# Half blocks for the experts' last tokens, a table laid over partitions, and new tile pools in a two-layer attention and mixture-of-experts kernel

## The chip, the cores and the metric

The kernel runs on one core of one Trainium2 chip. The metric is the device time in microseconds. Before the change three runs took 1161.4, 1163.57 and 1163.4 us, a median of 1163.4.

## What is computed

Two layers over `x` of 4 x 1024 tokens with 256 features, all in float32. The first adds causal attention and a dense feed-forward part. The second adds a grouped attention (with `qk`, `v`, a gate and rotated heads) and a mixture of 8 experts, of which each token takes 2. The part that the change is about, cut from the reference:

```python
scores = jax.nn.softmax(xf @ Wg.T, axis=-1)
expert_weights, expert_indices = jax.lax.top_k(scores, K)          # K = 2 of E = 8
expert_weights = expert_weights / expert_weights.sum(-1, keepdims=True)
gates = (jax.nn.one_hot(expert_indices, E) * expert_weights[..., None]).sum(axis=1)
h1 = _lora_in(xf, W1, b1, A1, B1)       # 256 -> 512
h3 = _lora_in(xf, W3, b3, A3, B3)       # 256 -> 512
g = jax.nn.silu(h1) * h3
y_e = _lora_out(g, W2, b2, A2, B2)      # 512 -> 256
y = jnp.einsum('te,ted->td', gates, y_e)
...
x = x + _L0_attn_ref(xn, ...) + _L0_ffn_ref(xn, ...)
xn = _layernorm(x, axis=-1)
x = x + _L1_attn_ref(xn, ...) + _L1_ffn_ref(xn, ...)
```

The kernel computes an expert only for the tokens routed to it: 8192 pairs of token and expert.

## The kernel before

The program has three stages in time. Names and lines are those of the profile.

**First layer** (0 to about 528 us): 16 units `u` of 256 tokens go through norms, `scores`, `hidden`, `weighted` and `finish`. Beside them `merge` folds each expert's low-rank parts into its weights, in DRAM (`wm13`, `wm2`). `norms` writes each unit's rows for the experts into a tile `xr` (five buffers of the pool `l0a`), `route` and `send` choose the two experts and each row's place, and `rows_out` (L641) has GpSimd scatter the rows from `xr` into `xg` in DRAM by indirect DMA, 64 of them; the last four are those of the last unit. Expert `e` owns rows `e * RS` and up of `xg`.

**Experts** (588 to 961 us): `table` (L736) counts each expert's tokens on all partitions at once, zeroes the 256 rows behind each expert's last one, and works out in a row of 39 numbers which expert (`etab`) and which rows (`rtab`) each block of `TB` = 256 tokens takes; it also turns each token's two ranks into its rows of the result (`slot1`, `slot2`). With 8192 pairs and 8 experts at most 39 blocks can be needed. `blocks` (L846) runs the first `NSURE` = 36 always and the last 3 under a branch on `live`. Per block, `rows` (L792) reads the row number into a register of ScalarE and fetches the tokens by four DMAs on ScalarE's queue, `weights` (L802) does so for the 1.7 MB of weights on SyncE's, `turn` (L810) transposes on VectorE, `up` (L815) and `down` (L836) multiply, and the result goes to `yg` in DRAM. The matmuls of block `i + 1`'s `up` stand ahead of those of block `i`'s `down`. In `up` the weights are stationary and the tokens stream, 256 columns a matmul; in `down` 128 tokens are stationary and the 256 columns of `w2` stream. A float32 matmul gives two records in the trace.

**Second layer's attention**, one batch of 1024 tokens after the other: `tokens` (L908) loads the normalised input, `heads` (L918) makes and rotates the four heads on VectorE, `values` (L950) and `gates` (L1012) multiply, `groups` (L967) transposes the heads and makes the attention matrices `attnT` and the linear part `linkv`, `gated` (L1034) combines them and `project` (L1061) ends it. Batch 0 runs ahead of the experts, between the first layer's last unit and the first block, with the tiles of pools named `tmp0`, `mid0`, `big0` and `late0`; batches 1 to 3 run behind the experts. `gather` has GpSimd fetch the expert results by `slot1` and `slot2`, `combine` adds them.

The order of the instructions is that of a scheduler that keeps the order of the program within what data, `issue_after` and buffers demand, engine by engine. A pool's tiles take the SBUF addresses of pools that were closed before; with `reuse_waits="tile"` a tile's first write then waits for whatever still uses the old tiles at its addresses, tile by tile. In `values` the matmuls of batch 0 go through two PSUM banks (`p_a`), and VectorE adds the bias and frees the bank.

Of the kernel before, what the change touches and what calls it, by code (L numbers as in the profile page):

```python
# [17 lines left out]
P = 128  # L18
# [33 lines left out]

TB = 256
RS = B * N + TB
NPAIR = 2 * B * N
NBLK = NPAIR // TB + E - 1

NSURE = NPAIR // TB + E // 2
# [4 lines left out]
def block_kernel(ctx: ExitStack, tc: tile.TileContext, x, wq, wk, wv, wfc, w1, w2, wqk, wvl, wg,  # L63
# [52 lines left out]
    for e in range(E):  # L116
# [9 lines left out]

    blkn = pers.tile([P, NBLK], F32, name="blkn")
    nc.gpsimd.iota(blkn, pattern=[[1, NBLK]], base=0, channel_multiplier=0,
                   allow_small_or_imprecise_dtypes=True)
    step = pers.tile([P, B * N // TB], F32, name="step")  # L130
    nc.gpsimd.iota(step, pattern=[[TB, B * N // TB]], base=0, channel_multiplier=0,
# [22 lines left out]
    etab = pers.tile([P, NBLK], I32, name="etab")  # L154
    rtab = pers.tile([P, NBLK], I32, name="rtab")
# [7 lines left out]
    yg = dram.tile([NBLK * TB, D], F32, name="yg")  # L163
# [60 lines left out]
    with ExitStack() as l0:  # L224
# [95 lines left out]
        def second(after):  # L320
            def load(eng, **k):
# [11 lines left out]

            load(nc.sync, out=yg[NSURE * TB :, :].rearrange("(k p) d -> p k d", p=P),
                 in_=zero.unsqueeze(1).to_broadcast([P, (NBLK - NSURE) * TB // P, D]))

# [397 lines left out]
    with ExitStack() as l1:  # L734

        def table():  # L736
# [10 lines left out]
            ns = B * N // TB  # L747
# [3 lines left out]
            nblk = small.tile([P, E], F32, tag="nblk", name="nblk", bufs=1)  # L751
            nc.vector.tensor_reduce(nblk, more, AX.X, ALU.add)
            upto = small.tile([P, E + 1], F32, tag="upto", name="upto", bufs=1)
            nc.vector.memset(upto[:, 0:1], 0.0)
            for e in range(E):
                nc.vector.tensor_tensor(upto[:, e + 1 : e + 2], upto[:, e : e + 1], nblk[:, e : e + 1], ALU.add)
            nc.vector.tensor_copy(live, upto[:, E : E + 1])

            by = [P, NBLK, E]
            past = tb.tile(by, F32, tag="past", name="past")  # L760
            nc.vector.tensor_tensor(past, blkn.unsqueeze(2).to_broadcast(by),
                                    upto[:, 1 : E + 1].unsqueeze(1).to_broadcast(by), ALU.is_ge)
            eblk = small.tile([P, NBLK], F32, tag="eblk", name="eblk", bufs=1)
            nc.vector.tensor_reduce(eblk, past, AX.X, ALU.add)
            nc.vector.tensor_scalar(eblk, eblk, float(E - 1), None, ALU.min)
            nc.vector.tensor_copy(etab, eblk)

            nc.vector.tensor_tensor(past[:, :, 0 : E - 1], past[:, :, 0 : E - 1],
                                    nblk[:, 0 : E - 1].unsqueeze(1).to_broadcast([P, NBLK, E - 1]), ALU.mult)
            rblk = small.tile([P, NBLK], F32, tag="rblk", name="rblk", bufs=1)  # L770
            nc.vector.tensor_reduce(rblk, past[:, :, 0 : E - 1], AX.X, ALU.add)
            nc.vector.tensor_tensor(rblk, blkn, rblk, ALU.subtract)
            nc.vector.tensor_scalar(eblk, eblk, float(RS), None, ALU.mult)
            nc.vector.scalar_tensor_tensor(rblk, rblk, float(TB), eblk, ALU.mult, ALU.add)
            nc.vector.tensor_scalar(rblk, rblk, tail[:, E - 1 : E], None, ALU.min)
            nc.vector.tensor_copy(rtab, rblk)
            start = small.tile([P, E], F32, tag="start", name="start", bufs=1)
            nc.vector.tensor_scalar(start, upto[:, 0:E], float(TB), None, ALU.mult)
            where = tb.tile([P, BT, E], F32, tag="wheres", name="where")
            nc.vector.tensor_tensor(where, rank, start.unsqueeze(1).to_broadcast([P, BT, E]), ALU.add)  # L780
            for oh, slot in ((oh1, slot1), (oh2, slot2)):
                at = tb.tile([P, BT, E], F32, tag="ats", name="at")
                nc.vector.tensor_tensor(at, oh, where, ALU.mult)
                fs = small.tile([P, BT], F32, tag="fsl", name="fs", bufs=1)
                nc.vector.tensor_reduce(fs, at, AX.X, ALU.add)
                nc.vector.tensor_copy(slot, fs)
# [4 lines left out]

        def rows(i):  # L792
            r = nc.scalar.value_load(rtab[0:1, i : i + 1], min_val=0, max_val=(E - 1) * RS + B * N)
            xt = exp.tile([P, DC, TB], F32, tag="xt", name="xt", bufs=3)
            src = xg[bass.ds(r, TB), :].rearrange("(i r) (c j a) -> j r c i a", r=32, c=DC, a=32)
            for j in range(4):
                got = nc.scalar.dma_start(out=xt[32 * j : 32 * j + 32].rearrange("r c (i a) -> r c i a", a=32), in_=src[j])
                for w in sent:
                    tc.add_manual_dep(got.ins, w.name, landed, reason="every row is in its slot")
            return xt  # L800

        def weights(i):  # L802
            e = nc.sync.value_load(etab[0:1, i : i + 1], min_val=0, max_val=E - 1)
            w13 = expw.tile([P, W13], F32, tag="w13", name="w13")
            nc.sync.dma_start(out=w13, in_=wm13[bass.ds(e, 1), :, :].rearrange("o p k -> p (o k)"))
            w2 = expw.tile([P, W2B], F32, tag="w2", name="w2")
            nc.sync.dma_start(out=w2, in_=wm2[bass.ds(e, 1), :, :].rearrange("o p k -> p (o k)"))
            return w13, w2

        def turn(xt):  # L810
            xT = exp.tile([P, DC, TB], F32, tag="xT", name="xT")
            nc.vector.transpose(xT, xt)
            return xT

        def up(xT, w13):  # L815
            g = exp.tile([P, EC, TB], F32, tag="g", name="g")
            for m2 in range(EC // 2):
                p1 = p_b.tile([P, 2, TB], F32, tag="b", name="p1")
                p3 = p_c.tile([P, 2, TB], F32, tag="c", name="p3")
# [6 lines left out]
                s = exp.tile([P, 2, TB], F32, tag="s", name="s")  # L826
# [3 lines left out]
                for j in range(2):  # L830
                    m = 2 * m2 + j
                    nc.vector.scalar_tensor_tensor(g[:, m, :], p3[:, j, :], w13[:, EB3 + m : EB3 + m + 1],  # L832
                                                   s[:, j, :], ALU.add, ALU.mult)
            return g

        def down(i, w2, g):  # L836
            yt = exp.tile([P, TB // P, D], F32, tag="yt", name="yt")
            py = p_d.tile([P, TB // P, D], F32, tag="d", name="py")
            for k in range(TB // P):
                for m in range(EC):  # L840
                    nc.tensor.matmul(py[:, k, :], g[:, m, ts(k, P)], w2[:, m * D : (m + 1) * D],  # L841
                                     start=(m == 0), stop=(m == EC - 1))
            nc.vector.tensor_tensor(yt, py, w2[:, EB2:W2B].unsqueeze(1).to_broadcast([P, TB // P, D]), ALU.add)  # L843
            nc.scalar.dma_start(out=yg[ts(i, TB), :].rearrange("(k p) d -> p k d", p=P), in_=yt)

        def blocks(i0, i1):  # L846
            last = None
            xts = {i: rows(i) for i in range(i0, min(i0 + 2, i1))}
            w13, w2 = weights(i0)
            xT = turn(xts.pop(i0))  # L850
            for i in range(i0, i1):
                if i + 2 < i1:
# [371 lines left out]
```

## Time and profile before

The profiled execution took 1163.01 us, 1161.3 us of it from the first to the last instruction; the granted clock was 0.999.

| what | value |
|---|---|
| median of three runs | 1163.4 us |
| the profiled execution | 1163.01 us |
| its span | 1161.3 us |
| VectorE, ScalarE, GpSimd busy | 47%, 26%, 15% |
| bytes moved | 149.52 MB, 129 GB/s over the span |
| TensorE waits for VectorE's `v` (the longest wait in total) | 3.9 us, in 4 pieces |

A line of the groups names the line of the program, the engine, the operation, what it writes and reads with its shape, how often it ran, its busy time and the mean of one, and the engine's idle time before it with what ended it. A line of the timeline begins with the start and the length in us. A line of stretches gives the busy time of the engines in the order PE, PEld, DVE, ACT, POOL, then TensorE's granted clock, the DMA engines' busy share and GB/s.

### The profile page before, as it was taken

What the parts mean: (1) busy time and instruction counts of PE and PEld (TensorE: products, weight loads), DVE (VectorE), ACT (ScalarE), POOL (GpSimd) and SP (SyncE); (2) the same over time, 40 slices, a digit from 0 to 9 for tenths busy, and PEclk for the clock granted to TensorE, in tenths of its full rate; (3) what the DMA queues carried; (4) which work ended last, traced back from release to release, by engine and by line L of the source; (5) the groups of instructions that cost most, each with busy time, mean ns of one, the idle gap of its engine ahead of it and who ended that gap; (6) DMA issues with size and microseconds to landing.
All of it is one profiled execution on the core that took longest, in us unless ns stands there. A gap on an engine that the chain in (4) does not pass through costs nothing. (4 is left out here: it accounts for less than half of the span.)

```text
span 1161.3 us, 15320 instructions
## 1 busy us (share of the span) xinstructions
PE 1142.0 (98%) x5308; PEld 896.7 (77%) x5308; DVE 547.1 (47%) x1486; ACT 303.7 (26%) x779; POOL 176.0 (15%) x209
## 2 busy tenths in 40 slices
PE   8999999999999999999999999999999999999997
PEld 6778878888878887874688888888888885554645
DVE  6442544345433344447663272232323324677855
ACT  3432333334323333225011121111111112122121
POOL 3200201123021213141000000000000003353410
PEclk9999999999999999999999999999999999999999
DMA  8510212232232232131658776677776642332211
GB/s 309 134 60 28 91 60 83 82 113 92 68 96 63 71 103 84 64 114 36 226 129 226 234 229 208 202 216 226 229 210 200 203 167 65 100 90 81 80 39 37
DMA packets 137552, 149.52 MB, mean 129 GB/s; under 512 B 84736, under 2 KB 109184, under 8 KB 132352
## 3 DMA queue, kind: packets, MB, share of 16 engines
q1 hardware_dynamic: 45360, 112.57, 29.0%
q10 hardware_dynamic: 85968, 19.15, 7.8%
q0 software_dynamic: 6144, 16.79, 4.6%
q8 instruction: 43, 0.70, 0.2%
q14 instruction: 37, 0.30, 0.1%
HBM read 107.84 MB, written 41.71 MB: 129 GB/s over the span
## 5 line engine op out<-in xcount | busy, mean ns | idle before, releaser
L824 PE MATMUL p<-xT,w 128*128 128x256 f32 x1152 | 254.6, 379 | 0.0
L824 PEld LDWEIGHTS p<-xT,w 128*128 128x128 f32 x1152 | 218.6, 190 | 30.3 <-issue 0.4
L829 ACT ACTIVATE s<-p,w 128x256 f32<-128x256 f32 x144 | 60.5, 471 | 332.3 <-PE p L824 317.6
L832 DVE SCALAR_TENSOR_TENSOR g<-p,w,s 128x256 f32<-128x256 f32 x144 | 62.9, 479 | 173.9 <-PE p L824 173.9
L883 POOL DMA_INDIRECT y<-yg,slot x64 | 65.1, 1017 | 510.5 <-PEq L868 429.4
L841 PE MATMUL py<-w,g 128*128 128x256 f32 x576 | 130.0, 379 | 0.0
L841 PEld LDWEIGHTS py<-w,g 128*128 128x128 f32 x576 | 109.4, 190 | 14.9
L480 PE MATMUL pm<-xnT,w_s 128*128 128x256 f32 x512 | 118.5, 379 | 0.0
L520 PE MATMUL po<-w_s,hT 128*128 128x256 f32 x512 | 116.1, 380 | 0.0
L520 PEld LDWEIGHTS po<-w_s,hT 128*128 128x128 f32 x512 | 96.8, 190 | 20.2 <-issue 8.0
L480 PEld LDWEIGHTS pm<-xnT,w_s 128*128 128x128 f32 x512 | 95.0, 190 | 11.6
L644 POOL DMA_INDIRECT xg<-xr,put x64 | 62.5, 976 | 167.2 <-ACT hT L483 75.7
L459 PE MATMUL sc<-xnT,qT 128*128 128x256 f32 (+1 forms) x320 | 65.8, 361 | 0.0
L504 PE MATMUL pz<-attT,xn 128*128 128x256 f32 (+1 forms) x320 | 65.0, 358 | 0.0
L504 PEld LDWEIGHTS pz<-attT,xn 128*128 128x128 f32 x320 | 57.1, 190 | 6.7
L958 PE MATMUL pv<-wvl_s,xl 128*128 128x512 f32 x128 | 57.6, 597 | 4.0 <-DVE v L960 3.9
L524 PE MATMUL pv<-vo_s,zT 128*128 128x512 f32 x128 | 60.2, 592 | 0.0
L459 PEld LDWEIGHTS sc<-xnT,qT 128*128 128x128 f32 x320 | 54.6, 191 | 6.0 <-ACT qT L446 0.2
L1076 PE MATMUL pj<-wo_s,gd 128*128 128x256 f32 x256 | 57.0, 381 | 1.1 <-DVE o L1078 0.6
L1029 PE MATMUL pg<-xl,wg_s 128*128 128x512 f32 x128 | 57.5, 593 | 0.0
L483 ACT ACTIVATE hT<-pm,colt 128x256 f32<-128x256 f32 x128 | 52.6, 466 | 13.9 <-PE pm L480 13.6
L843 DVE TENSOR_TENSOR yt<-py,w 128x512 f32<-128x512 f32 x36 | 24.9, 691 | 64.8 <-PE py L841 64.8
(226 smaller groups left out, 1315.3 us busy)
## 6 DMA issues: line engine op xcount, KB each, us to landing
w<-wm SPq DMA_DIRECT2D x36, 1028.0 KB
w<-wm SPq DMA_DIRECT2D x36, 640.0 KB
wt<-in_ew_dram SPq DMA_DIRECT2D x16, 768.0 KB
xt<-xg ACTq DMA_DIRECT2D x144, 64.0 KB
yg<-yt ACTq DMA_DIRECT2D x36, 256.0 KB
wm<-wt SPq DMA_DIRECT2D x16, 512.0 KB
wm<-wt SPq DMA_DIRECT2D x16, 256.0 KB
out_dram<-x SPq DMA_DIRECT2D x15, 256.0 KB
```

The lines of the kernel that those rows point to most:

```text
L459: nc.tensor.matmul(sc[:, kp * 2 * P : kp * 2 * P + w], qT[:, c, ts(i, P)], xnTs[b * NP + kp][:, c, 0:w], start=(c == 0), stop=(c == DC - 1))
L480: nc.tensor.matmul(pm[:, j, :], w1_s[:, c, ts(2 * m2 + j, P)], xnTs[u][:, c, :], start=(c == 0), stop=(c == DC - 1))
L504: nc.tensor.matmul(pz[:, c, q0:], xns[b * NP + j // 2][:, j % 2, ts(c, P)], attT[:, j, q0:], start=(j == 0), stop=(j == last))
L520: nc.tensor.matmul(po[:, i, :], hT[:, m, ts(i, P)], w2_s[:, m, :], start=(m == 0), stop=(m == IC - 1))
L524: nc.tensor.matmul(pv, zT[:, c, ts(i, P)], vo_s[:, c, :, :], start=(c == 0), stop=(c == DC - 1))
L644: w = nc.gpsimd.indirect_dma_start(out=xg, out_offset=bass.IndirectOffsetOnAxis(ap=put[:, b * NT + t : b * NT + t + 1], axis=0), in_=xrs[b ...
L824: nc.tensor.matmul(p[:, j, :], w13[:, w0 : w0 + P], xT[:, c, :], start=(c == 0), stop=(c == DC - 1))
L829: nc.scalar.activation(s[:, j, :], p1[:, j, :], AF.Silu, bias=w13[:, EB1 + m : EB1 + m + 1])
L832: nc.vector.scalar_tensor_tensor(g[:, m, :], p3[:, j, :], w13[:, EB3 + m : EB3 + m + 1], s[:, j, :], ALU.add, ALU.mult)
L841: nc.tensor.matmul(py[:, k, :], g[:, m, ts(k, P)], w2[:, m * D : (m + 1) * D], start=(m == 0), stop=(m == EC - 1))
L883: w = nc.gpsimd.indirect_dma_start(out=ys[b][:, t, k, :], out_offset=None, in_=yg, in_offset=bass.IndirectOffsetOnAxis(ap=slot[:, n : n + ...
L958: nc.tensor.matmul(pv, a.xl[:, c, ts(t, P)], wvl_s[:, c, :], start=(c == 0), stop=(c == DC - 1))
```

## The change

An expert's tokens are cut into whole blocks of 256 and, where at least one and at most 128 tokens are left over, one half block of 128 (`HB`). There are `NF` = 32 whole blocks and up to 7 halves; 4 halves (`NSURE`) are always run, one after every seventh whole block, and 3 under the branch. Where an expert order leaves fewer than 32 whole blocks, two halves share a whole block's place.

`table` puts block `i` on partition `i`, so that `etab` and `rtab` are one column, and each number is read by a register read of its own just ahead of its DMAs, held behind the DMAs of the block before. The slots are worked out in a function of their own (`slots`) behind the `up` of block 3. The first two blocks' rows, weights and the first transpose are asked for ahead of `project(0)`, from the pool `expw`, which now also holds `xt`, `xT` and a third `w13`. `w2` is fetched at its block's start, `w13` two blocks ahead. The loads of `xl` stand behind block 3's weights, `heads(1)` behind block 3's `up`, `values(1)` behind the last `down`. The pools of the second layer's attention get an additional `post` (for `attnT`, `plks`, `sim`, `linkv`, `gate`) and another order.

```diff
 TB = 256
+HB = TB // 2
-NBLK = NPAIR // TB + E - 1
-NSURE = NPAIR // TB + E // 2
+NF = NPAIR // TB
+NHB = E - 1
+NBLK = NF + NHB
+NSURE = E // 2
...
-    etab = pers.tile([P, NBLK], I32, name="etab")
-    rtab = pers.tile([P, NBLK], I32, name="rtab")
+    etab = pers.tile([P, 1], I32, name="etab")
+    rtab = pers.tile([P, 1], I32, name="rtab")
...
-    yg = dram.tile([NBLK * TB, D], F32, name="yg")
+    yg = dram.tile([NF * TB + NHB * HB, D], F32, name="yg")
...
-            upto = small.tile([P, E + 1], F32, tag="upto", name="upto", bufs=1)
-            nc.vector.memset(upto[:, 0:1], 0.0)
-            for e in range(E):
-                nc.vector.tensor_tensor(upto[:, e + 1 : e + 2], upto[:, e : e + 1], nblk[:, e : e + 1], ALU.add)
+            nc.vector.tensor_reduce(odd, more, AX.X, ALU.add)
+            nc.vector.tensor_reduce(whole, more.rearrange("p e (s k) -> p e s k", k=2)[:, :, :, 1], AX.X, ALU.add)
+            nc.vector.scalar_tensor_tensor(odd, whole, -2.0, odd, ALU.mult, ALU.add)
+            nc.vector.tensor_scalar(whole, whole, 2.0, None, ALU.mult)
+            nc.vector.tensor_copy(size, whole)
+            for k in range(4):
+                nc.vector.tensor_tensor(run[1 - k % 2][:, E:], run[k % 2][:, E:], run[k % 2][:, E - 2 ** k : 3 * E - 2 ** k], ALU.add)
...
+        def slots(after):
+            first, half, room = table.slots
+            every = [P, BT, E]
+            where = exp.tile(every, F32, tag="wheres", name="where", bufs=1)
+            with tc.issue_after(after):
+                nc.vector.tensor_tensor(where, rank, room.unsqueeze(1).to_broadcast(every), ALU.is_ge)
+            nc.vector.tensor_tensor(where, where, half.unsqueeze(1).to_broadcast(every), ALU.mult)
+            nc.vector.tensor_tensor(where, where, first.unsqueeze(1).to_broadcast(every), ALU.add)
+            nc.vector.tensor_tensor(where, where, rank, ALU.add)
...
+        def wide(i):
+            return TB if i < NF else HB
+
         def rows(i):
-            r = nc.scalar.value_load(rtab[0:1, i : i + 1], min_val=0, max_val=(E - 1) * RS + B * N)
-            xt = exp.tile([P, DC, TB], F32, tag="xt", name="xt", bufs=3)
+            n = wide(i)
+            with tc.issue_after(rows.last) if rows.last else nullcontext():
+                r = nc.scalar.value_load(rtab[i : i + 1, 0:1], min_val=0, max_val=(E - 1) * RS + B * N)
+            xt = expw.tile([P, DC, n], F32, tag="xt", name="xt", bufs=3)
...
         def weights(i):
-            e = nc.sync.value_load(etab[0:1, i : i + 1], min_val=0, max_val=E - 1)
-            w13 = expw.tile([P, W13], F32, tag="w13", name="w13")
-            nc.sync.dma_start(out=w13, in_=wm13[bass.ds(e, 1), :, :].rearrange("o p k -> p (o k)"))
-            w2 = expw.tile([P, W2B], F32, tag="w2", name="w2")
-            nc.sync.dma_start(out=w2, in_=wm2[bass.ds(e, 1), :, :].rearrange("o p k -> p (o k)"))
-            return w13, w2
+            with tc.issue_after(weights.last) if weights.last else nullcontext():
+                e = nc.sync.value_load(etab[i : i + 1, 0:1], min_val=0, max_val=E - 1)
+            w13 = expw.tile([P, W13], F32, tag="w13", name="w13", bufs=3)
+            weights.last = nc.sync.dma_start(out=w13, in_=wm13[bass.ds(e, 1), :, :].rearrange("o p k -> p (o k)")).ins
+
+            def rest():
+                w2 = expw.tile([P, W2B], F32, tag="w2", name="w2")
+                nc.sync.dma_start(out=w2, in_=wm2[bass.ds(e, 1), :, :].rearrange("o p k -> p (o k)"))
+                return w2
+            return w13, rest
...
+        def prepare(order):
+            xts = {i: rows(i) for i in order[0:2]}
+            ws = {i: weights(i) for i in order[0:2]}
+            return xts, ws, turn(xts.pop(order[0]), wide(order[0]))
+
+        def blocks(order, ahead):
             last = None
-            xts = {i: rows(i) for i in range(i0, min(i0 + 2, i1))}
-            w13, w2 = weights(i0)
-            xT = turn(xts.pop(i0))
-            for i in range(i0, i1):
-                if i + 2 < i1:
-                    xts[i + 2] = rows(i + 2)
-                if i + 1 < i1:
-                    nxt = weights(i + 1)
-                g = up(xT, w13)
+            xts, ws, xT = ahead
+            for k, i in enumerate(order):
+                w13, rest = ws.pop(i)
+                w2 = rest()
+                if k + 2 < len(order):
+                    xts[order[k + 2]] = rows(order[k + 2])
+                    ws[order[k + 2]] = weights(order[k + 2])
+                g = up(xT, w13, wide(i))
+                if i == 3:
+                    tokens.after = weights.last
+                    slots(up.g)
+                    heads.after = up.g
...
-        def experts():
-            more = nc.values_load(live[0:1, 0:1], min_val=0, max_val=NBLK)
-            blocks(0, NSURE)
+        def experts(ahead):
+            more = nc.values_load(live[0:1, 0:1], min_val=0, max_val=NHB)
+            order, halves = [], list(range(NF, NF + NSURE))
+            for i in range(NF):
+                order.append(i)
+                if i % 7 == 6 and halves:
+                    order.append(halves.pop(0))
+            blocks(order, ahead)
+            values.after = down.last
             with tc.If(more > NSURE):
...
-            a.attnT = mid.tile([P, NT, P], F32, tag="attnT", name="attnT")
+            a.attnT = post.tile([P, NT, P], F32, tag="attnT", name="attnT")
...
-                tmp, mid, big, late = (pool(st, n) for n in ("tmp0", "mid0", "big0", "late0"))
+                tmp, mid, late, big, post = (pool(st, n) for n in ("tmp0", "mid0", "late0", "big0", "post0"))
...
                 gated(0)
+                ahead = prepare((0, 1))
                 project(0)
             exp = ex.enter_context(tc.tile_pool(name="exp", bufs=2, reuse_waits="tile"))
-            experts()
-        late, gat, mid, big, tmp = (pool(l1, n) for n in ("late", "gat", "mid", "big", "tmp"))
+            experts(ahead)
+        late, gat, post, mid, big, tmp = (pool(l1, n) for n in ("late", "gat", "post", "mid", "big", "tmp"))
```

## The prediction, made before the changed kernel was run

> **What bounds the kernel now.** I read the busy shares first, then the expert groups, then TensorE in order of time, then the waits.
>
> ```profile
> PE 1142.0 (98%) x5308; PEld 896.7 (77%) x5308; DVE 547.1 (47%) x1486; ACT 303.7 (26%) x779; POOL 176.0 (15%) x209
> ...
> L824 PE MATMUL p<-xT,w 128*128 128x256 f32 x1152 | 254.6, 379 | 0.0
> ...
> L841 PE MATMUL py<-w,g 128*128 128x256 f32 x576 | 130.0, 379 | 0.0
> ```
>
> TensorE works 98% of the span, so only fewer or shorter matmuls, or new holes, move the time. `up` has 1152 records over 32 a block: 36 blocks are run, `NSURE`, and the branch behind them is not taken. The timeline gives one block's price:
>
> ```profile
> 926.93 7.07 PE L824 MATMUL p<-xT,w 128*128 128x256 f32 x32
> ...
> 933.84 3.62 PE L841 MATMUL py<-w,g 128*128 128x256 f32 x16
> ...
> 937.29 7.07 PE L824 MATMUL p<-xT,w 128*128 128x256 f32 x32
> ```
>
> From start to start: `up` 933.84 - 926.93 = 6.91 us, `down` 3.45 us, a block 10.36 us, 0.216 us per record of 256 columns (379 ns is a record's length in the pipe). 36 x 10.36 = 373.0 us fills 588.3 to 961.5 without a hole. The stretches of that stage (engine columns, then granted clock, DMA share, GB/s) leave room elsewhere:
>
> ```profile
> 900.00:910.36 10.36, 10.36 (x50) 9.12 (x49) 3.06 (x8) 1.68 (x4) 0.00 (x0) 1.00 0.71 218
> 588.30:961.50 373.20, 373.20 (x1730) 328.06 (x1729) 130.00 (x260) 62.13 (x147) 0.00 (x0) 1.00 0.69 207
> ```
>
> **Half blocks.** Counting the reference's routing gives 1073, 1335, 1318, 932, 1010, 1056, 447 and 1021 tokens: 36 blocks of 256 as the trace has, or 32 whole blocks and 4 halves. That is what runs now without the branch (32 + 4 kept), so four full blocks become four halves. TensorE's order is otherwise the same, instruction for instruction. A half's `down` has 8 records of 256 columns: 1.73 us. Its `up` keeps 32 records and 32 weight loads, each with 128 columns. The nearest row is `gated`'s product with `attnT`, same load and same 128 columns:
>
> ```profile
> 560.37 1.86 PEld L1055 LDWEIGHTS po<-attnT,v 128*128 128x128 f32 x16 [0.76 <-DVE attnT L1003]
> ```
>
> Sixteen loads in 1.86 us, the last lasting 0.19: (1.86 - 0.19)/15 = 0.111 us apart. So `up` 32 x 0.111 = 3.56, a half 5.29, and the change saves 4 x (10.36 - 5.29) = **20.3 us**. The low end, if loads cannot overlap at all, is in the rivals.
>
> **Weights and rows under the halves: nothing.** A half still fetches 1028 + 640 KB. Seven full blocks and a half move 7 x 2.23 + 1.97 = 17.6 MB in 77.8 us of TensorE, 226 GB/s, where 218 now takes a DMA share of 0.71. With three `w13` buffers a block's `w13` is asked for two blocks ahead (14 us at the least, round a half) and `w2` about 13; before it was 8.9 us. Should that cover go, each late block costs what its weights are late.
>
> **Register reads: nothing.** Before, ScalarE's queue read 31 row starts in a run (from 558.7) and asked for the first rows only at 578.57; SyncE likewise held `xl` until 585.67. Yet the first `up` matmul at 588.30 follows `project` with no hole, so there is nothing to gain. One by one each read is 0.277 + 0.147 + 0.018 = 0.44 us on a ScalarE that has 1.68 us of work in 10.36. One read moves ahead of `linkv`: that copy now waits for `rtab`. Adding up the new table (count to `rtab`: 44 instructions, two of 0.69 us, three of 0.3 to 0.4, the rest 0.1 apart where independent and 0.2 where chained, as in the old table) puts `rtab` near 557.2, against 558.66; the first read took 0.76 us plus 0.17, so `linkv` starts at 558.2, not 557.95. TensorE waits for `linkv` already: **+0.3 us**, between 0 and 1.7 (small instructions at 0.14 apart).
>
> **Rows and transposes pulled ahead of `project`: nothing.** The first transpose now stands on VectorE before the last two `gd` products. Behind `linkv` come three `qk` Silus (1.9 us) and four row DMAs (0.78 each); the zero rows they wait for are issued until 561.6, so rows land near 569, while that place on VectorE is reached near 571. Late, it would hold the `gd` products and then `pj`.
>
> **Slots, heads, `xl` moved into the experts: nothing.** Ten slot instructions (some 3.5 us) and `heads(1)` (13 us) stand on VectorE over blocks 3 to 6, where it has 7 us free in each 10.36; the `g` behind them has about 6 us before its PSUM bank is wanted. Both `xl` loads (2 MB) now queue on SyncE ahead of `w2` of block 4: 7 us of traffic against 13 to 17 us of lead. `values(1)` already stood behind the last `down`; the hold changes no order.
>
> **The pools laid out anew: a stall.** This is the part that costs. In the built program `big0`'s `v` now lies over the last two `xr` tiles, so the first addition into `v` in `values(0)` waits for the last eight row scatters to land; before, `v` lay elsewhere and those waits stood at `heads(1)`, deep in the experts. Where things are now:
>
> ```profile
> 530.60 1.28 DVE L960 TENSOR_TENSOR v<-pv,rowt 128x512 f32<-128x512 f32 x2
> ...
> 532.93 10.46 PE L958 MATMUL pv<-wvl_s,xl 128*128 128x512 f32 x24
> ...
> 535.20 0.96 POOL L644 DMA_INDIRECT xg<-xr,put  x1 [0.30 <-issue]
> ```
>
> and, by stretches, the DMA traffic that they leave (last two columns):
>
> ```profile
> 536.50:537.50 1.00, 1.00 (x4) 0.44 (x3) 1.00 (x3) 0.19 (x1) 0.00 (x0) 1.00 0.36 131
> 537.50:540.00 2.50, 2.50 (x7) 1.14 (x6) 2.50 (x6) 1.26 (x2) 0.00 (x0) 1.00 0.00 0
> ```
>
> GpSimd issues the last scatter at 535.2; DMA traffic stops at 537.5 (the share is 0.00 after). So `v` starts near 537.7 instead of 530.60 and ends its first tile at 538.4. `pv` has two banks, both filled by then, so the 24 `pv` records that began at 532.93 begin at 538.5: **+5.5 us** of idle TensorE. Behind `v` on VectorE stand all of `heads(0)` and the table: 17.3 us of work with 0.2 of memsets, from 537.7 to 555.2, while TensorE, resumed, reaches the `r` transposes 17.3 us later at 555.8. So nothing is added; all that follows shifts by 5.5. [...]
>
> [...] The end of the trace shows what idling does to the clock (last matmul ends at 1155.8):
>
> ```profile
> 1155.80:1158.00 2.20, 0.00 (x1) 0.00 (x0) 2.14 (x7) 0.96 (x4) 0.00 (x0) 1.00 0.34 116
> 1158.00:1159.50 1.50, 0.00 (x0) 0.00 (x0) 0.48 (x1) 0.03 (x1) 0.00 (x0) 1.00 0.28 94
> 1159.50:1160.20 0.70, 0.00 (x0) 0.00 (x0) 0.00 (x0) 0.00 (x0) 0.00 (x0) 0.77 0.52 173
> 1160.20:1161.30 1.10, 0.00 (x0) 0.00 (x0) 0.00 (x0) 0.00 (x0) 0.00 (x0) 0.50 0.02 7
> ```
>
> The clock halves some 4.1 us after the last matmul (0.77 over 0.7 us is 0.32 us at half). [...] The longest hole before is 1.6 us at a clock of 1.00, so the trace cannot price a return. [...]
>
> **After the experts: nothing.** Orders are unchanged; `late`, `gat` and `post` overlap expert buffers whose last use is over by the time they are written (`plks` waits for the last `yg` stores, 16 us old). [...]
>
> **Sum**, against the profiled execution's 1163.0 us (span 1161.3 and 1.7 around it; the median of the runs is 1163.4): -20.3 + 5.5 + 1.5 + 0.3 = -13.0, so **1150 us**.
>
> **Rivals.**
> *Weights too late (slower).* The place is SyncE's weight stream round the halves. Four groups must lose the 13.0 gained, 3.25 us each: 81.1 us for 17.6 MB, so it turns slower if the DMA engines give under 217 GB/s. At the stage's mean of 207 a group lasts 85.0 us, 7.2 lost, 29 in all: 1179 us. For it: 211 to 226 GB/s is all that the stage ever moved. Against: no `up` waits for a weight in the trace, the share is 0.7, and 10 to 20 us moved 354 GB/s at full share.
> *Weight loads bind.* If loads follow each other at their own 190 ns, `up` of a half is 6.08 us, the saving 4 x 2.55 = 10.2: 1160 us. For it the mean of every load row; against it the 0.111 spacing.
> *No stall.* If the scatters land before `v` needs them or TensorE has something to run, -20.0: 1143 us. Against it is the GpSimd row at 535.20.
> *The branch is taken.* Expert 7, at 1021, is three tokens below needing a fifth half; then three halves (15.9 us) and an empty pipeline (some 8) make about 1174.
>
> **Numbers.** The sum as it stands 0.76; weights late 0.08 (with the branch 0.09); loads bind 0.05; no stall 0.10. Its own range is 1146 to 1155: the stall's -1.0 to +1.5, the clock's -1.5 to +1.9, the read's -0.3 to +1.4, and 1.7 for 128-column records at 0.124 instead of 0.111, not all at once. Down to 1143 for the case without a stall gives 1143 to 1157. About 0.2% (2.3 us) is what a measurement tells from no change: faster (under 1161.1) 0.88, same 0.03, slower 0.09.
>
> **What would show it.** Right: 1024 `up` records of 256 columns and 128 of 128 about 0.111 apart; 4 halves near 5.3 us; no wait of `up` or `py` for DMA; a hole of 5 to 6 us before `pv` put down to `v` or a DMA, with a clock under 1.00 just behind it; `linkv` a few tenths later. Wrong: a hole at the start of the block after a half, or none before `pv`.

## The result and the profile after

The changed kernel took 1152.45 us (median of six runs, 1151.31 to 1157.32), the kernel before it on the same chip 1162.81 us (six runs). The ratio is 0.9922, with an interval of 0.9905 to 0.994, that is 9.1 us less (7.0 to 11.1; the two medians are 10.4 apart). In a second set the ratio was 0.9924 (0.991 to 0.9937). The prediction was 1150 us, 13 less than the profiled run of before, with a range from 1143 to 1157.

The profiled execution took 1155.08 us, 1153.4 of it span. First the page of it, busy shares and two groups:

```profile
PE 1127.4 (98%) x5276; PEld 884.5 (77%) x5276; DVE 543.9 (47%) x1506; ACT 302.0 (26%) x779; POOL 176.6 (15%) x216
...
L896 PE MATMUL p<-xT,w 128*128 128x256 f32 (+1 forms) x1152 | 241.0, 367 | 0.0
...
L915 PE MATMUL py<-w,g 128*128 128x256 f32 x544 | 123.1, 379 | 0.0
```

By form, the records of 128 columns:

```profile
L896 PE MATMUL p<-xT,w 128*128 128x128 f32 x128 | 14.9, 275 | 0.0
```

`up` still has 1152 records, 128 of them, 32 for each of four halves, in this form. `down` has 544 instead of 576: 32 fewer, eight for each of four halves. TensorE is still busy for 98% of a shorter span. Its timeline around one half block (start, length, engine, what it writes and reads, records):

```profile
672.70 3.73 PE L896 MATMUL p<-xT,w 128*128 128x128 f32 x32
676.27 3.62 PE L915 MATMUL py<-w,g 128*128 128x256 f32 x16
679.73 7.07 PE L896 MATMUL p<-xT,w 128*128 128x256 f32 x32
686.64 1.89 PE L915 MATMUL py<-w,g 128*128 128x256 f32 x8
688.36 3.83 PE L896 MATMUL p<-xT,w 128*128 128x256 f32 x17
```

From start to start the half's `up` takes 676.27 - 672.70 = 3.57 us, its `down` 688.36 - 686.64 = 1.72: 5.29 us for a half.

TensorE's timeline between the first layer and the experts, where the rest of the difference lies:

```profile
532.35 3.68 PE L1122 MATMUL pg<-xl,wg_s 128*128 128x512 f32 x8
541.36 13.44 PE L1051 MATMUL pv<-wvl_s,xl 128*128 128x512 f32 x24 [5.33 <-DVE v L1053]
...
561.50 0.28 PE L750 MATMUL pn<-seen,ones 128*128 128x8 f32 x2
...
570.15 1.13 PE L1144 MATMUL po<-qlT,linkv 64*128 64x512 f32 x4 [0.84 <-ACT linkv L1101]
...
586.51 5.88 PE L1169 MATMUL pj<-wo_s,gd 128*128 128x256 f32 x26 [0.29 <-DVE gd L1150]
594.95 8.85 PE L1169 MATMUL pj<-wo_s,gd 128*128 128x256 f32 x32 [2.56 <-DVE o L1171]
603.64 8.58 PE L896 MATMUL p<-xT,w 128*128 128x256 f32 x39
```

The bracket is the idle time before a group and what ended it. There is a hole of 5.33 us before `pv`, and the 24 `pv` records behind it take 13.44 us, where the same 24 took 10.46 before. A second hole of 2.56 us stands in `project`, where before had none of that size:

```profile
573.92 10.53 PE L1076 MATMUL pj<-wo_s,gd 128*128 128x256 f32 x48
584.74 3.72 PE L1076 MATMUL pj<-wo_s,gd 128*128 128x256 f32 x16 [0.30 <-DVE o L1078]
```

Reading the same TensorE instructions in every profile cuts the program into six stretches: to the second group of gate matmuls (`pg`), from there to the count matmul (`pn`), to the first `po`, to the first `up`, to the first `pv` behind the experts, and to the end. All are in us:

| profile | to `pg` | `pg`-`pn` | `pn`-`po` | `po`-`up` | `up`-`pv` | `pv`-end |
|---|---|---|---|---|---|---|
| before | 529.42 | 20.68 | 8.49 | 29.71 | 373.17 | 199.83 |
| before, second profile (`before_again`) | 529.81 | 20.69 | 8.49 | 30.04 | 374.16 | 199.81 |
| after | 532.35 | 29.15 | 8.65 | 33.49 | 352.72 | 197.04 |
| after, second profile (`after_again`) | 531.04 | 28.96 | 8.69 | 33.14 | 352.72 | 199.75 |

Against the first profile of before, the experts give -20.45, the stretch with the hole costs +8.3 to +8.5, `linkv` +0.2 and `project` +3.4 to +3.8. These four make -8.0 in the first profile of after and -8.5 in the second, against 8.8 and 9.1 less measured. Against the second profile of before, in which TensorE waits once for `yt` in the experts (0.73 us), they make -9.4 and -9.9, of which the experts give -21.44. The first and the last stretch are taken up below.

What VectorE, ScalarE and GpSimd did at the hole and at the transposes, from the timeline of after:

```profile
538.12 0.96 POOL L656 DMA_INDIRECT xg<-xr,put  x1 [0.30 <-issue]
540.61 1.29 DVE L1053 TENSOR_TENSOR v<-pv,rowt 128x512 f32<-128x512 f32 x2 [6.99 <-DMA xg<-xr,put]
541.45 1.28 ACT L1056 ACT_TABLE_LOAD   x1 [8.78 <-DVE v L1053]
...
544.74 0.61 ACT L1013 ACTIVATE qk<-qk 128x512 f32<-128x512 f32 x1
...
545.39 1.23 DVE L1021 TENSOR_TENSOR hd<-qk,hg_s 128x1024 f32<-128x1024 f32 x1 [3.46 <-ACT qk L1013]
546.53 0.68 DVE L1053 TENSOR_TENSOR v<-pv,rowt 128x512 f32<-128x512 f32 x1
...
585.17 0.71 DVE L884 STREAM_TRANSPOSE xT<-xt 128x512 f32<-128x512 f32 x1 [3.40 <-DMA xt<-xg]
...
593.27 0.71 DVE L884 STREAM_TRANSPOSE xT<-xt 128x512 f32<-128x512 f32 x1 [3.41 <-DMA xt<-xg]
```

The first `v` addition waits for the scatters of rows, and starts 2.5 us after the last of them was issued. ScalarE had waited for that `v`: only behind it come a table load, Silus and the `qk` Silu, and `hd` on VectorE waits for this. The third `v` addition stands behind `hd`. At the transposes VectorE waits 3.4 us twice for rows.

By stretches (engine columns, then TensorE's granted clock, the DMA engines' busy share and GB/s):

```profile
603.64:956.36 352.72, 352.72 (x1698) 312.21 (x1697) 126.74 (x267) 58.76 (x144) 0.00 (x0) 1.00 0.69 215
...
540.00:545.00 5.00, 3.64 (x5) 1.58 (x6) 1.32 (x4) 3.54 (x5) 0.00 (x0) 0.53 0.00 0
545.00:550.00 5.00, 5.00 (x11) 2.17 (x10) 4.61 (x6) 3.72 (x6) 0.00 (x0) 0.78 0.00 0
```

In the experts TensorE is never idle. Behind the hole the clock is at one half until 547.18, for 5.8 us.

### The profile page after: what moved, and what is told of

It reads as the page before. It is cut to its first block, busy times and chain, and to the rows that moved or that the text cites. A ratio compares the mean times of both kernels' runs of the same rounds, so it can differ in the third digit from the quotient of the medians.

```text
span 1153.4 us, 15284 instructions
## 1 busy us (share of the span) xinstructions
PE 1127.4 (98%) x5276; PEld 884.5 (77%) x5276; DVE 543.9 (47%) x1506; ACT 302.0 (26%) x779; POOL 176.6 (15%) x216
## 5 line engine op out<-in xcount | busy, mean ns | idle before, releaser
L896 PE MATMUL p<-xT,w 128*128 128x256 f32 (+1 forms) x1152 | 241.0, 367 | 0.0
L896 PEld LDWEIGHTS p<-xT,w 128*128 128x128 f32 x1152 | 209.5, 190 | 26.7
L901 ACT ACTIVATE s<-p,w 128x256 f32<-128x256 f32 (+1 forms) x144 | 58.8, 459 | 318.4 <-PE p L896 248.2
L904 DVE SCALAR_TENSOR_TENSOR g<-p,w,s 128x256 f32<-128x256 f32 (+1 forms) x144 | 60.9, 463 | 161.8 <-PE p L896 159.4
L915 PE MATMUL py<-w,g 128*128 128x256 f32 x544 | 123.1, 379 | 0.0
L915 PEld LDWEIGHTS py<-w,g 128*128 128x128 f32 x544 | 103.1, 190 | 13.8
L492 PEld LDWEIGHTS pm<-xnT,w_s 128*128 128x128 f32 x512 | 95.0, 190 | 11.6
L1051 PE MATMUL pv<-wvl_s,xl 128*128 128x512 f32 x128 | 60.3, 621 | 7.5 <-DVE v L1053 7.2
L1169 PEld LDWEIGHTS pj<-wo_s,gd 128*128 128x128 f32 x256 | 49.2, 195 | 11.4 <-DVE o L1171 4.0
## 6 DMA issues: line engine op xcount, KB each, us to landing
wm<-wt SPq DMA_DIRECT2D x16, 512.0 KB, 2.8
```

Of the source, the lines that this page charges most:

```text
L492: nc.tensor.matmul(pm[:, j, :], w1_s[:, c, ts(2 * m2 + j, P)], xnTs[u][:, c, :], start=(c == 0), stop=(c == DC - 1))
L896: nc.tensor.matmul(p[:, j, :], w13[:, w0 : w0 + P], xT[:, c, :], start=(c == 0), stop=(c == DC - 1))
L904: up.g = nc.vector.scalar_tensor_tensor(g[:, m, :], p3[:, j, :], w13[:, EB3 + m : EB3 + m + 1], s[:, j, :], ALU.add, ALU.mult).ins
L915: down.last = nc.tensor.matmul(py[:, k, :], g[:, m, ts(k, P)], w2[:, m * D : (m + 1) * D], start=(m == 0), stop=(m == EC - 1)).ins
L1051: nc.tensor.matmul(pv, a.xl[:, c, ts(t, P)], wvl_s[:, c, :], start=(c == 0), stop=(c == DC - 1))
L1169: nc.tensor.matmul(pj, a.gd[:, m, ts(n, P)], wo_s[:, m, :], start=(m == 0), stop=(m == HC - 1))
```

## The experiments

Each is an edit of the changed kernel. Ratios are to the kernel before on the same chip.

### v clear of the row scatters

```diff
-tmp, mid, late, big, post = (pool(st, n) for n in ("tmp0", "mid0", "late0", "big0", "post0"))
+tmp, mid, big, late, post = (pool(st, n) for n in ("tmp0", "mid0", "big0", "late0", "post0"))
```

> Only the order of the first-stage pools is changed (big0 below late0), so that v no longer lies over xr; the instructions and their order stay. If the wait of v for the last row scatters is the whole cause of what is lost between the gates' matmuls and the count matmul pn, the 5.3 us hole goes and the 24 pv records behind it take 10.5 us instead of 13.4: 8.5 us less than the changed kernel, about 1144 us. If the slow pv records have a cause of their own: 5.3 us less, about 1147. If the scatters are waited for further down anyway (the row fetch needs them landed), the time comes back there: 0 to 3 us less.

It took 1148.03 us, ratio 0.9852 (0.9836 to 0.9868). TensorE's timeline of `e1_v_clear`:

```profile
530.85 3.68 PE L1122 MATMUL pg<-xl,wg_s 128*128 128x512 f32 x8
534.36 10.46 PE L1051 MATMUL pv<-wvl_s,xl 128*128 128x512 f32 x24
...
551.53 0.28 PE L750 MATMUL pn<-seen,ones 128*128 128x8 f32 x2
...
585.74 8.69 PE L1169 MATMUL pj<-wo_s,gd 128*128 128x256 f32 x32 [3.10 <-DVE o L1171]
```

There is no hole before `pv`, its records take 10.46 us as before the change, and `pg` to `pn` is 551.53 - 530.85 = 20.68 us, to the hundredth what it was. Apart from two row fetches deep in the experts that changed places with a Silu on ScalarE's queue, and a few waits on semaphores, no instruction changed its place on any engine; only the addresses did. So the whole loss of this stretch came from where `v` lay, and little of it returned later: the wait in `project` is 3.10 us, and `po` to `up` 34.07, 0.6 to 0.9 more than in the changed kernel.

### What makes the pv records slow: the clock, or the chain behind v

The 3.0 us on top of the hole had two candidates, the lowered clock and the chain through ScalarE. Two edits remove one each, a third both.

```diff
+            busy.last = gate_sum.last
...
+                if b == 0 and t == 1:
+                    for k in range(6):
+                        pw = p_d.tile([P, H1], F32, tag="d", name="pw")
+                        with tc.issue_after(busy.last):
+                            busy.last = nc.tensor.matmul(pw, a.xl[:, k % 2, 0:P], wvl_s[:, k % 2, :], start=True, stop=True).ins
```

> Six additional matmuls without a use (12 records of 512 columns, 5.2 us) stand between the second gate matmuls and the third pv; the wait of v stays. If the lowered clock alone makes the 24 pv records behind the hole 3.0 us longer: 3.0 us less, about 1149.5, and the clock stays at 1.00. If the chain on VectorE and ScalarE alone does (the third v addition stands behind hd, which waits for the qk Silu behind a table load and the Silus of v and gd): TensorE waits for a pv bank instead, and no more than 0.3 us is gained. If the additional matmuls hold up the pv: some tenths more.

```diff
-                with tc.issue_after(heads.after) if b == 1 else nullcontext():
+                with tc.issue_after(heads.after) if b == 1 else tc.issue_after(a.pace[3]) if b == h == 0 else nullcontext():
```

> The first head product hd is held behind the fourth v addition, so that no v addition waits for the qk Silu; the wait of v for the scatters stays, and so does the hole. Read from the second gate matmuls to pn, 28.96 to 29.15 us until now. If the lowered clock behind the hole alone binds: 29. If the chain on ScalarE and VectorE alone binds: 26. If both set the same time one beside the other: 29 here, and 26 only in e7_hd_held_busy.

> The edits of e4_busy and e6_hd_held together: neither a lowered clock nor a v addition behind the qk Silu. If these two are all that lengthens the 24 pv records behind the hole, they take 10.5 us in a run and the stretch from the second gate matmuls to pn 26.0 us (20.7 and the hole of 5.3). If something else holds them, 27.5 to 29.

TensorE's timeline of `e4_busy`:

```profile
533.57 5.31 PE L1063 MATMUL pw<-wvl_s,xl 128*128 128x512 f32 x12
539.07 3.70 PE L1055 MATMUL pv<-wvl_s,xl 128*128 128x512 f32 x8 [0.19 <-DVE v L1057]
544.98 7.32 PE L1055 MATMUL pv<-wvl_s,xl 128*128 128x512 f32 x16 [2.21 <-DVE v L1057]
```

The hole is filled and the first eight `pv` records run at full speed, 3.70 us. Then TensorE waits 2.21 us for a `v` addition, the one behind `hd`. With both edits, `e7_hd_held_busy`:

```profile
539.71 10.57 PE L1055 MATMUL pv<-wvl_s,xl 128*128 128x512 f32 x24 [0.19 <-DVE v L1057]
```

| `pg` to `pn`, us | `hd` as it was | `hd` held back |
|---|---|---|
| hole left empty | 28.96 (`after_again`) | 28.55 (`e6_hd_held`) |
| hole filled | 28.96 (`e4_busy`) | 26.29 (`e7_hd_held_busy`) |

Either edit alone gains 0.0 and 0.4 us, both together 2.7. The clock and the chain stood side by side: the clock alone costs 28.55 - 26.29 = 2.3 us, the chain alone 28.96 - 26.29 = 2.7, and the longer one is what one sees. What the clock costs depends on where the half rate ends: in `e6_hd_held` it lasts 4.5 us behind the hole, half of which is the 2.3; in the first profile of after it lasts 5.8, which would be 2.9 (an estimate), and there the stretch is 29.15. In time, `e4_busy` took 1153.48 us, 0.9914 (0.9896 to 0.9932), not to be told from the changed kernel; `e6_hd_held` and `e7_hd_held_busy` were timed once (1157.16 and 1152.16 us), and the `hd` edit also moved `linkv` behind a register read (`pn` to `po` 9.8 us), so only the one stretch is read from them.

### The transposes ahead of project

`e2_turns_later` leaves rows and weights where the change has put them and moves the two transposes; `e3_rows_first` leaves the transposes and holds the weights.

```diff
-            return xts, ws, turn(xts.pop(order[0]), wide(order[0]))
+            return xts, ws, None
...
+            with tc.issue_after(at[0].pace[-3]) if order[0] == 0 else nullcontext():
+                xT = turn(xts.pop(order[0]), wide(order[0]))
...
-                    xT = turn(xts.pop(order[k + 1]), wide(order[k + 1]))
+                    with tc.issue_after(at[0].pace[-1]) if i == 0 else nullcontext():
+                        xT = turn(xts.pop(order[k + 1]), wide(order[k + 1]))
```

> The first two transposes are held behind the sixth and the eighth o addition of project(0); rows and weights are still asked for ahead of project. If the cost of the early prefetch is that VectorE stands at a transpose whose rows are late, with gd and o queued behind it: the 0.3 and 2.6 us waits of pj and the slow clock behind them go, 3.0 to 3.8 us less, about 1149. If TensorE needs those rows at that time anyway, the wait moves to the first up: no gain, 1152.5.

```diff
             weights.last = nc.sync.dma_start(out=w13, in_=wm13[bass.ds(e, 1), :, :].rearrange("o p k -> p (o k)")).ins
+            if i < 2:
+                tc.add_manual_dep(weights.last, rows.last.name, landed, reason="rows first")
```

> The w13 loads of the first two blocks wait until the rows of the second block have landed; nothing else is moved. If the rows are late because they share the DMA engines with 3.3 MB of weights, they land some 5 us after they are asked for (as before the change) instead of 10.6, the waits of VectorE go, and the time falls by 3 to 3.8 us, to about 1149. If row fetches in pieces of 128 bytes are slow by themselves, the transposes wait as now and the time stays. If the weights then come too late for the first up at about 600 us, it rises by what they are late, some 2 to 5 us.

They took 1151.42 us (0.9887, 0.9871 to 0.9902) and 1151.06 us (0.9878, 0.9863 to 0.9892). In both, `project`'s 64 records run in one piece of 13.98 us, and `po` to `up` falls to 28.4 us: 4.7 to 5.1 less than in the changed kernel, more than was expected, and 1.3 less than before the change. So it is VectorE's place at a transpose whose rows are late that costs, and not the rows themselves, which TensorE did not need yet.

Why were they late? The stretches of `after_again`, where the rows are asked for at 573.0 us:

```profile
574.00:578.00 4.00, 4.00 (x24) 2.56 (x23) 1.38 (x2) 0.00 (x0) 0.00 (x0) 1.00 1.00 404
578.00:582.00 4.00, 4.00 (x24) 2.56 (x23) 1.38 (x2) 0.00 (x0) 0.00 (x0) 1.00 1.04 316
```

and of `e3_rows_first`, where they are asked for at 572.9:

```profile
574.00:578.00 4.00, 4.00 (x24) 2.56 (x23) 1.38 (x2) 0.00 (x0) 0.00 (x0) 1.00 0.42 66
578.00:582.00 4.00, 4.00 (x24) 2.56 (x23) 2.00 (x3) 0.00 (x0) 0.00 (x0) 1.00 0.44 69
```

The DMA engines are full (share 1.00, 404 GB/s) in the one and under half busy in the other. VectorE's timeline of `e3_rows_first` shows what that does:

```profile
580.11 0.70 DVE L886 STREAM_TRANSPOSE xT<-xt 128x512 f32<-128x512 f32 x1
...
587.65 0.69 DVE L886 STREAM_TRANSPOSE xT<-xt 128x512 f32<-128x512 f32 x1
```

No wait stands before them; in `after_again` they run at 583.48 and 591.51, after waits of 3.2 and 3.3 us. The weights' traffic makes the rows late, not the rows' own small pieces. (Asked for by then were two `w13` and one `w2`, 2.8 MB, not the 3.3 of the expectation.) Held behind the rows, the weights still come in time: no `up` waits for them.

### Both losses taken away

> The edits of e1_v_clear and e3_rows_first together: v clear of the row scatters, and the first two w13 loads behind the rows. If the two losses are independent, they add up: pg to pn 20.7 us, pn to the first up 37.1 us, 13.5 us less than the changed kernel (8.5 and 5.0), a ratio near 0.981 to the kernel before. If one hides the other (with the stall gone the rows are late against an earlier project), no more than e1 or e3 alone with 0.985.

It took 1144.33 us (1143.2 to 1144.55), ratio 0.9818 (0.9806 to 0.9831): the losses are independent, as expected. TensorE's timeline of `e5_clear_rows_first`:

```profile
535.93 10.46 PE L1053 MATMUL pv<-wvl_s,xl 128*128 128x512 f32 x24
...
576.37 13.98 PE L1171 MATMUL pj<-wo_s,gd 128*128 128x256 f32 x64
590.19 13.98 PE L898 MATMUL p<-xT,w 128*128 128x256 f32 x64
```

`pg` to `pn` is 20.68 us and `po` to `up` 28.43. With these two edits the new kernel is 1.8% faster than before, where the change as made gives 0.8%.

### Halves and their weights

```diff
-NSURE = E // 2
+NSURE = E - 1
...
-                if i % 7 == 6 and halves:
+                if i % 4 == 3 and halves:
...
-            with tc.If(more > NSURE):
...
```

> All seven halves are run always, the three that hold no token too, one after every fourth whole block; the branch and the zeroing of the rest of the results are left out. If a half costs its 128-column records, 0.111 us apart, and nothing else: 3 x 5.29 = 15.9 us more between the first up and the first pv behind the experts, 352.7 to 368.6. If weight loads bound it, 7.8 us a half: 23. If the weights came late where a half follows every fourth block, waits of up or py for a DMA appear and it is more than 16.

```diff
-                if i % 7 == 6 and halves:
-                    order.append(halves.pop(0))
+            order += halves
```

> The four halves run one after the other behind the 32 whole blocks; the work is the same. Each asks for 1.67 MB in 5.29 us, 315 GB/s, where the stage moves 218 to 226. If the spacing of the halves is what keeps the weights hidden: the lead of 14 us shrinks by some 1.5 to 2.5 us with each half, and the last two or three wait, 2 to 6 us more in all. If the DMA engines give more when asked (354 GB/s early in the program), nothing: 352.7 us from the first up to the first pv.

`e8_seven_halves` took 1172.0 us (ratio 1.0063, 1.0046 to 1.008). Its experts' stretch is 368.62 us, 15.90 more for three halves: 5.30 each. Its records by form:

```profile
L894 PE MATMUL p<-xT,w 128*128 128x128 f32 x224 | 26.1, 275 | 0.0
```

The last number is TensorE's idle time before all 224 of them: none, though a half now follows every fourth block. `e9_halves_last` took 1156.57 us (0.9929, 0.9913 to 0.9946), no different from the changed kernel, and its stretch is again 352.72 us. Its halves on TensorE:

```profile
938.20 3.73 PE L896 MATMUL p<-xT,w 128*128 128x128 f32 x32
941.77 1.89 PE L915 MATMUL py<-w,g 128*128 128x256 f32 x8
943.50 3.73 PE L896 MATMUL p<-xT,w 128*128 128x128 f32 x32
947.07 1.89 PE L915 MATMUL py<-w,g 128*128 128x256 f32 x8
```

From start to start 943.50 - 938.20 = 5.30 us a half, one behind the other without a gap. I had expected a loss if the spacing mattered; it doesn't. From 940 to 950 us the DMA engines gave 276 GB/s.

### Each kernel once more

> The changed kernel once more, without an edit, beside the others. If the 2.8 us that its profile was shorter behind the experts belong to the change, they are there again: 197.0 us from the first pv behind the experts to the end. If they are a gap in VectorE's instruction supply that one profile had and another had not: 199.7 us, as in the kernel before. Its ratio to the kernel before again 0.990 to 0.994.

> The kernel before once more, for a second profile of it. If the first 530 us differ between the two kernels only by what one execution happens to have (a slow clock between 22 and 30 us), the second gate matmuls start somewhere between 529.4 and 532.4 here too. If the changed kernel's start is longer by itself, they start at 529.4 again, and the changed kernel's 530.0 to 532.4 count as a loss of 0.6 to 3. The four other stretches should repeat: 20.7, 8.5, 29.7, 373.2 and 199.8 us.

From the first `pv` behind the experts to the end, the second profile of the changed kernel has 199.75 us, and every edited one 199.2 to 199.8. In twelve of the thirteen profiles, both of before among them, VectorE stands for 2.93 or 2.94 us ahead of one `r` product of the heads and waits for nothing that the profile shows ("issue"); only the first profile of after lacks this gap. So the 2.8 us are not the change's. Why one profile lacks the gap stays open.

The first stretch is 529.4 and 529.8 us in the two profiles of before, and 530.0 to 532.4 in the eleven of the changed and edited kernels. Most of this is the clock. In nine of the eleven it goes to one half between 21.5 and 23.1 us, behind a hole of 1.59 us that every profile has and that ends at 20.2 to 21.0. From the end of that hole to `pg` it takes 509.0 to 510.1 us in the four profiles that keep the full clock (both of before, `e4_busy`, `e7_hd_held_busy`), 510.5 to 510.7 in seven that have 3.41 us at half rate, and 512.0 in two that have 6.83 us. Which of these an execution gets goes with the moment at which its clock first rises: 4.5 to 6.0 us after the start in the nine, 6.2 to 7.5 in the four. The kernel before meets it too: seven of its 30 timed runs beside these experiments have a mean clock of 0.996 or 0.997, which is at least 5.8 us at half rate, and the span behind its last matmul is only 5.5 us long. So this part is no cost that the change alone has; whether the changed kernel meets it more often is not shown.

## Why the prediction was right, and where it was not

The direction and the range were right, and the largest term was right within 0.2 us. The sum was 4 to 5 us too good, in two terms. That the time still lay in the range is in part luck: no bound was set aside for a wait in `project`, and what it cost was taken up by bounds that stood for the stall, the clock and the reads. (The low end, 1146, is below what those bounds give: 1150 - 1.0 - 1.5 - 0.3 = 1147.2.)

**Half blocks: -20.3 predicted, -20.45 measured** against the first profile of before (-21.44 against the second, with its wait for `yt`). The price from the nearest row, 0.111 us a record at 128 columns, came out as 3.57 / 32 = 0.112. Loads did not bind at 190 ns.

**Weights and rows under the halves: nothing, and nothing was measured.** No `up` waits in any expert stage of the changed and edited kernels. The rival with late weights took 207 to 226 GB/s for what the DMA engines can give; it was what they were asked for. In `e9_halves_last` they gave 276 when asked.

**Slots, heads and `xl` in the experts: nothing, and nothing was measured.** 32 x 10.36 + 4 x 5.29 = 352.7 us is the whole stretch of 352.72.

**Register reads and `linkv`: +0.3 predicted, +0.2 measured.** `pn` to `po` went from 8.49 to 8.65 and 8.69.

**The stall of `v`: +5.5 predicted, 5.33 measured.** In the frame of before the first addition was put at 537.7 us; it ran at 540.61, less the 2.93 by which the first stretch was longer, 537.68. The cause was right: `e1_v_clear` moves only addresses, and the hole is gone. The -1.0 to +1.5 that the range allows the stall was the author's estimate; in the seven profiles that keep this wait and leave the hole empty (both of after, `e2_turns_later`, `e3_rows_first`, `e6_hd_held`, `e8_seven_halves`, `e9_halves_last`) it is 5.33 to 5.35 us long.

**What stands behind `v`: "nothing is added", 1.5 for the clock. 3.0 us was measured; this term was too small.** The prediction followed VectorE's queue behind `v` and found its total work no longer than TensorE's. It did not follow ScalarE's, which stood still for 8.78 us for the same `v`; its table load and Silus came before the `qk` Silu that `hd` needs, and `hd` stood ahead of the third `v` addition. The 1.5 for the clock in the sum was the author's estimate, and no run shows that term; what the runs showed in its place is a clock at one half for 4.5 us (`e6_hd_held`) to 5.8 us (the first profile of after) behind the hole, 2.3 us by itself in `e6_hd_held`. This is within the 0 to 3.4 that the range allows the clock (1.5 - 1.5 to 1.5 + 1.9). Had the clock stayed full, the chain would have cost 2.7.

**Rows and transposes pulled ahead of `project`: nothing predicted, +3.4 to +3.8 measured. This is the step that failed.** The prediction saw the danger ("late, it would hold the `gd` products and then `pj`") and judged it by one number: rows landing near 569, VectorE at the place near 571. Shifted by the 11.6 us by which the three stretches ahead were longer, that is 582.6 for the place and 580.6 for the rows. The place was right: VectorE was free at 581.8. The rows came at 585.2. Their flight had been taken from the zero rows' end without the two `w13` and the first `w2`, which the same change asks for at the same moment (573.5 to 575.8); the first row DMAs were asked for at 574.53 and took 10.6 us, where before, asked for at 578.57 in light traffic (a DMA share of 0.26, 42 GB/s, from 578 to 582 us), they took 5:

```profile
583.60 0.71 DVE L812 STREAM_TRANSPOSE xT<-xt 128x512 f32<-128x512 f32 x1 [0.79 <-DMA xt<-xg]
```

The waits of `pj` are only part of the price, 0.3 and 2.6 us; behind the second hole the clock was at one half for 3.4 us. With the wait gone, `po` to `up` fell by 4.7 to 5.1, to less than before the change, so the +3.4 to +3.8 is what was left of a larger loss.

**After the experts: nothing, and nothing was measured**, once the gap that one profile lacks is known.

## What to carry to other kernels

When pools are laid out anew, list for each tile's first write what last used its addresses, and then follow every queue that stands behind that write, not only the queue of the engine that writes. When a loss has two possible causes, remove both as well as each: here each alone gained next to nothing and the two together 2.7 us. A prefetch that is moved forward takes its own big transfers along; let the small one that somebody waits for in order land first, and the big ones, which have time, behind it.

## What the runs showed of the hardware

The clock went down behind holes of 2.49 and of 1.59 us. The second profile of the changed kernel has a hole of 2.49 us in `project` that ends at 593.19. Its stretches there:

```profile
589.69:593.10 3.41, 1.01 (x5) 0.56 (x3) 1.56 (x4) 0.00 (x0) 0.00 (x0) 1.00 0.37 58
593.10:596.52 3.42, 3.33 (x8) 2.70 (x9) 2.88 (x11) 0.00 (x0) 0.00 (x0) 0.50 0.47 75
```

Around the hole of 1.59 us near the start, the first profile of after:

```profile
18.11:21.52 3.41, 1.57 (x11) 0.92 (x10) 3.20 (x13) 1.72 (x6) 0.00 (x0) 1.00 1.12 380
21.52:24.94 3.42, 2.85 (x9) 2.10 (x9) 2.79 (x11) 1.95 (x7) 0.20 (x1) 0.50 1.01 408
```

and the first of before, where the clock stays full:

```profile
19.83:23.24 3.41, 2.02 (x11) 1.38 (x12) 3.41 (x14) 1.73 (x6) 0.00 (x0) 1.00 1.08 383
```

In the first profile of after the clock first rises at 4.46 us and changes at 21.52, 28.35, 540.35, 547.18, 594.96 and 598.38 us; from one change to the next it is 5, 2, 150, 2, 14 and 1 times 3.413 us. In the first profile of before it rises at 6.17 us and stays full until behind the last matmul. The stretches just shown of these two profiles begin a whole number of times 3.413 us after the rise. With both profiles cut in this way from the rise to the last matmul, the stretches just ahead of the three falls in after held 1.57 us of matmuls (from 18.11), 0.00 (from 536.94) and 0.85 (from 591.55); every other stretch at the full clock held 2.0 us or more, in before as in after. In after the hole of 1.59 us near the start (18.76 to 20.35) lies within one such stretch; in before (18.80 to 20.38) it is divided between two, of 2.39 and 2.02 us of matmuls. So the same hole was followed by half rate in the one and not in the other, and that is how the moment of the first rise comes to matter above.

One DMA issue took long by itself: beside the weights, one of the first four row DMAs held ScalarE's queue for 3.4 us in both profiles of the changed kernel, with a median of 0.61 over 20, and so put off every later one. In before none of the first 21 took more than 0.85 us. In `e3_rows_first`, where the weights come behind the rows, the median of 22 is 0.60 and the longest 4.1 us, and none of the three transposes up to 610 us waited for its rows.
